# Values, queries and keys by fifteen products on thirds, in a two-layer graph kernel on one core

## The chip, the core and the metric

The kernel runs on one core of a Trainium2 chip. TensorE (PE) multiplies matrices into PSUM; VectorE (DVE) and ScalarE (ACT) read PSUM and do the element-wise work; GpSimd (POOL) does further sums in SBUF; SyncE (SP) issues most of the loads. The metric is the time of one execution on the device in microseconds (us).

## The reference, cut to what matters

The input is x of 128 graphs with 64 nodes and 768 features, and a 0/1 adjacency matrix adj of each graph. All arithmetic is in fp32. Layer 0 mixes three linear maps of the nodes by a masked attention; layer 1 is an attention with twelve heads of 64 features. Both end in a residual and a layer norm:

```python
def layer0(h, adj):
    attn = softmax(h @ h.T / sqrt(d)) * adj        # per graph; rows divided by their sums
    ctx = triu(attn, 1) @ (h @ Wl.T + bl) + diag(attn) * (h @ Ws.T + bs) + tril(attn, -1) @ (h @ Wr.T + br)
    return relu(layernorm(ctx, 1e-12) * gamma + beta)

def layer1(h, adj):
    q, k, v = (split_heads(h @ W + b) for W, b in ((Wq, bq), (Wk, bk), (Wv, bv)))
    s = q @ k.T / sqrt(64) + beta1 * adj
    s = where(adj > 0, s, -9e15)
    return merge_heads(softmax(s) @ v)

x = layernorm(x + layer0(x, adj))
x = layernorm(x + layer1(x, adj))
```

The change touches how q, k and v are computed, and how the heads are grouped in the scores and the weighted sums.

## The kernel before

**Blocks and stages.** The 8192 nodes are cut into 16 blocks of 512 tokens (8 graphs). The main loop (L1030 to L1157) runs over n. In one turn it does layer 0 of block m = n + 1, layer 1 of block n, and the end of layer 1 of block p = n - 1, which lags by one turn. TensorE's stages of a turn, in order, are: the left and right maps of block m (`both_sides`, L620, from block 3 on; "deep" below), its self map (`self_part`), then the values of block n (`values`, L774), then queries and keys of block n for three groups of four heads (`projected`, L794).

**Seven products.** A product of a 512x768 and a 768x768 matrix is done with seven products of halves in place of eight (`seven`, L370), by sums and differences of the halves of tokens and of the weights. Each of the seven is three matmuls (K is 384) for each of two halves: for the values over 128 tokens with 384 columns, for a group of queries or keys over 128 features with 256 token columns. Products accumulate in PSUM chains of the tags X and Y, two banks each; what is read halfway is kept in `u` and added at a later read. The left and right maps of deep blocks apply this twice: 49 sub-products, most of one or two matmuls of 384 columns (`nested`, L425).

**Places and queues.** Nothing is scheduled automatically: the order of every engine's instructions is the order in which the program issues them. Each product of a stage is a place; `hooks` names functions that run ahead of it. The deep stage has 28 places spread over its 49 sub-products (`left` 0 to 13, `right` 14 to 27). After each product `step` (L137) takes waiting items from three queues: `first` goes before `urgent`, that before `lazy`, and one plain item is taken per step. Items marked act or gap may come along without using that up. In the deep stage the steps behind sub-products 5, 1 and 3 of each seven are light, and take no plain item. `settle(key)` (L163) issues at once everything that is still queued up to the last item with that key; `freed` (L158) issues all that is left in `first`.

**Layer 1's attention.** `scores` (L822) issues the score matmuls of a group, multiplies by the mask on VectorE, and queues under the key ("e", n, group): adding the bias, the row maximum, lowering by it (each on 128x1024), then sixteen exponentials of 32x256 on ScalarE, and two transposes of 128x512 on VectorE. `weighted` (L876) settles that key, issues the product of the probabilities with the values, and queues four additions under ("y", n, group) in `first`. Each addition is one reciprocal and four multiply-adds of 128x64. `finish` (L907) settles ("y", n, 0) and ("y", n, 1), and queues the layer norm (L945, L946). Groups 0 and 1 have their scores within the stage of queries and keys (of group 1 and group 2); group 2 has them in the next turn's deep stage, at left 2. The weighted sums come in group 2's stage (group 0), at left 5 (group 1) and at right 1 (group 2); `finish` is at right 2.

**Loads.** Weights of the self, left, right and value stages and of queries and keys go through one ring of 19 buffers (`wst`), 192 KB each. SyncE issues a load where its product is issued in the program, so a load goes out as soon as its buffer has been read, up to 19 buffers ahead of TensorE. ScalarE issues the four loads `sq<-x1d` (L301), which bring layer 0's output back in a transposable order.

Of the kernel before, what the change touches and what calls it, by code (L numbers as in the profile page):

```python
# [17 lines left out]
P = 128  # L18
# [5 lines left out]
T = 4  # L24
# [7 lines left out]
NHG = HC  # L32
# [17 lines left out]

@with_exitstack
def gnn_two_layers(ctx: ExitStack, tc, x, adj, wl, bl, ws, bs, wr, br, gamma, beta,
# [8 lines left out]
    s_p = ctx.enter_context(tc.tile_pool(name="s_p", bufs=1))  # L61
    s2_p = ctx.enter_context(tc.tile_pool(name="s2", bufs=2))
    l0 = ctx.enter_context(tc.tile_pool(name="l0", bufs=1))
    l0t = ctx.enter_context(tc.tile_pool(name="l0t", bufs=T))
    tmp = ctx.enter_context(tc.tile_pool(name="tmp", bufs=2))
    wst = ctx.enter_context(tc.tile_pool(name="wst", bufs=19))
# [106 lines left out]
    qk_d = tc.dram_tile([NHG, 7, P, 2, HC, P], F32, name="qk_d")  # L173
# [23 lines left out]

    def prepare(nm, quarter_pool, sum_pool, waits=(0, 0, 0), queue=lazy):
# [7 lines left out]
        for q in ((0, 0), (1, 0), (0, 1), (1, 1)):  # L206
            b[q] = chunks(quarter_pool, f"b{q[0]}{q[1]}_{nm}")

            with tc.issue_after(streamed["l"][8]) if nm == "k" else ExitStack():
                move(nc.sync, b[q][1], b[q][0], source=src[q])  # L210
# [3 lines left out]
        if nm in "slrv":  # L214
            d = tc.dram_tile([4, P, HC, HALF], F32, name=f"d_{nm}")
            pieces[nm] = {1: src[0, 0], 2: src[1, 0], 3: src[1, 1], 5: d[0], 6: d[1], 7: d[2], 4: d[3]}

        def store(i):
            if nm in "slrv":
                if i in (5, 6, 7, 4):  # L220
                    move(nc.gpsimd, in_sbuf[i][1], in_sbuf[i][0], to=pieces[nm][i])
            else:


                engine, first = (nc.sync, streamed["s"][20]) if nm == "q" else (nc.gpsimd, last_sum[1].ins)
                with tc.issue_after(first):
                    for hg in range(NHG):
                        engine.dma_start(out=qk_d[hg, i - 1, :, "qk".index(nm)],
                                        in_=in_sbuf[i][1][:, :, hg * P : (hg + 1) * P])
# [25 lines left out]
        if nm in "qk":  # L255
            later(key, lambda: store(1), lambda: store(2), lambda: store(3), queue=queue)
# [60 lines left out]
    def combined(xT, n=None):  # L317

        a11, a12 = xT[:, 0:HC, 0:HTOK], xT[:, HC:KC, 0:HTOK]
        a21, a22 = xT[:, 0:HC, HTOK:NTOK], xT[:, HC:KC, HTOK:NTOK]  # L320
        s1, s2 = (s_p.tile([P, HC, HTOK], F32, tag=f"S{i}", name=f"S{i}") for i in (1, 2))
        nc.gpsimd.tensor_tensor(s1, a21, a22, ALU.add)  # L322
        nc.gpsimd.tensor_tensor(a21, a11, a21, ALU.subtract)
        S = {1: a11, 2: a12, 4: a22, 5: s1, 6: s2, 7: a21}
        if n is not None and n >= DEEP:

            S["deep"] = {i: second_level(S[i]) for i in ORDER2[:2]}
        nc.gpsimd.tensor_tensor(s2, s1, a11, ALU.subtract)
        return S

    def combined4(S, n=None):

        S[3] = s_p.tile([P, HC, HTOK], F32, tag="S4", name="S4")
        last_sum[n] = nc.gpsimd.tensor_tensor(S[3], S[2], S[6], ALU.subtract)

# [265 lines left out]

    def side_part(n, nm, in_sbuf, hooks={}):
# [3 lines left out]
        if nm == "l":  # L606
            blk["lr"] = [l0t.tile([P, 2, D], F32, tag="lr", name=f"lr_{n}_{t}") for t in range(T)]
# [12 lines left out]
    def both_sides(n, hooks):  # L620
# [4 lines left out]
        lr = blk["lr"] = [l0t.tile([P, 2, D], F32, tag="lr", name=f"lr_{n}_{t}") for t in range(T)]  # L625
# [20 lines left out]
        def view(ps):  # L646
            return ps[:, 0:HALF].rearrange("p (s c) -> p s c", s=2)

        C = {(m, n_): {(a, b): lr[2 * m + a][:, :, n_ * HALF + b * QUAD : n_ * HALF + (b + 1) * QUAD]
                       for a in range(2) for b in range(2)} for m in range(2) for n_ in range(2)}  # L650
# [4 lines left out]
        def swapped(t):  # L655
            low, high = lr[t][0:L, 1, :], lr[t][L:P, 0, :]
            swap = l1s_p.tile([P, T * 4 * L], F32, tag="s", name="swap")
# [6 lines left out]
    def context0(n):  # L664
# [8 lines left out]
        def unused():  # L673
            return l1s_p.tile([P, T * 4 * L], F32, tag="s", name="unused")[:, 0:D]
# [99 lines left out]
    def values(n, hooks={}, stay=False):  # L774

        def pairs(a):
            return a.rearrange("p (j r d) -> p r j d", r=2, d=HD)  # L780

        def last(t, h, ps, part):
            add = pairs(bias["v"][:, h * HALF : (h + 1) * HALF] if part is None else part)
            heads = slice(h * 3, (h + 1) * 3)
            nc.vector.tensor_tensor(v[:, t, :, heads, 0:HD], pairs(ps), add, ALU.add)

        by_tokens("v", blocks[n]["S"], last, None, hooks)
        if not stay:
            low, high = v[0:L, :, 1, :, 0:HD], v[L:P, :, 0, :, 0:HD]
            swap = l0t.tile([P, T, HP, HD], F32, tag="lr", name="swap")  # L790
# [3 lines left out]
    def projected(n, hg, hooks={}):  # L794

        blk = blocks[n]
        S = blk["S"]
        qk = [l1_p.tile([P, 2, NTOK], F32, tag=nm, name=nm) for nm in "qk"]
        wt = {}

        def factors(i, j):
            w = wst.tile([P, HC, P], F32, tag="w", name="wqk")
            nc.sync.dma_start(out=w, in_=qk_d[hg, i - 1, :, j])
            return [(w[:, k, :], S[i][:, k, :]) for k in range(HC)]

        def first(j, b, ps, kept):
            u = tmp.tile([P, HALF], F32, tag="u1" if kept else "u0", name="uqk")[:, 0:HTOK]
            c = b * HC + hg
            nc.scalar.activation(u, ps, AF.Identity, bias=bias["qk"[j]][:, c : c + 1])  # L809
            return u  # L810

        def last(j, m, h, ps, part):
            dst = qk[j][:, h, m * HTOK : (m + 1) * HTOK]
            if part is None:
                nc.scalar.activation(dst, ps, AF.Identity, bias=bias["qk"[j]][:, h * HC + hg : h * HC + hg + 1])  # L815
            else:
                nc.vector.tensor_tensor(dst, ps, part, ALU.add)  # L817

        seven(HTOK, factors, first, last, hooks, True)
        blk["qk"] = qk  # L820

    def scores(n, hg, at_once=1, pool=None, gaps=1):  # L822


# [3 lines left out]
        q, k = blk["qk"]  # L828
# [4 lines left out]
        s = l1s_p.tile([P, T * 4 * L], F32, tag="s", name="s").rearrange("p (t c r m) -> p t c r m", t=T, c=2, r=2)  # L833
        sc = [ps_mm.tile([P, T, 2, L], F32, tag="mm", name=f"sc{r}") for r in range(2)]
        for t in range(T):
            for c in range(2):
                for r in range(2):
                    rows = slice(r * HD, (r + 1) * HD)
                    for g in range(2):
                        tok = slice(t * P + g * L, t * P + (g + 1) * L)  # L840
                        nc.tensor.matmul(sc[r][g * L : (g + 1) * L, t, c, :], lhsT=q[rows, c, tok],  # L841
                                         rhs=k[rows, c, tok], start=True, stop=True)
        m8, add = blk["m8"], blk["add"]
        for r in range(2):
            nc.vector.tensor_tensor(s[:, :, :, r, :], sc[r], m8[:, :, None, :].to_broadcast([P, T, 2, L]), ALU.mult)
# [3 lines left out]
        mx = st.tile([P, T * 4], F32, tag="mx1", name="mx1")  # L849

        def exponentials(groups):
            if 0 in groups:
                blk["eT", hg] = (pool or l1e_p).tile([P, T, 2, P], F32, tag="lr" if pool else "eT", name="eT")
            e = blk["eT", hg].rearrange("p t c i -> p (t c) i")
# [8 lines left out]
        def turn(h):  # L863
            e = blk["eT", hg][:, h * 2 : h * 2 + 2].rearrange("p t c i -> p (t c i)")
            nc.vector.transpose(e, e)

        later(("e", n, hg),
              lambda: nc.vector.tensor_tensor(s4, s4, add[:, :, None, :].to_broadcast([P, T, 4, L]), ALU.add),
              lambda: nc.vector.tensor_reduce(mx, s8, AX.X, ALU.max),
              lambda: nc.vector.tensor_tensor(s8, s8, mx[:, :, None].to_broadcast([P, T * 4, L]), ALU.subtract),  # L870
              *(part for a in range(0, P // Q, at_once) for part in
                (act(partial(exponentials, range(a, a + at_once))), *([GAP] if hg == 1 and a == 0 else []))),
# [3 lines left out]
    def weighted(n, hg):  # L876
# [4 lines left out]
        settle(("e", n, hg))  # L881
        freed()
        xt, eT = blk["x"], blk["eT", hg]
        y = {(r, h): ps_mm.tile([P, 2, 2, HD + 1], F32, tag="mm", name=f"ps_y{r}") for h in range(2) for r in range(2)}
        for h in range(2):
            for t in range(2):
                for c in range(2):
                    for r in range(2):
                        rows = slice(r * L, (r + 1) * L)
                        for g in range(2):  # L890
                            cols = slice(g * L, (g + 1) * L)
                            nc.tensor.matmul(y[r, h][cols, t, c, :], lhsT=eT[rows, 2 * h + t, c, cols],  # L892
                                             rhs=v[rows, 2 * h + t, g, hg + c * HC, :], start=True, stop=True)

        def added(h, r):
            ps = y[r, h]
            rz = st.tile([P, 2, 2], F32, tag="rz1", name="rz1")
            nc.vector.reciprocal(rz, ps[:, :, :, HD])
            for t in range(2):
                res = xt[2 * h + t].rearrange("p (c k r d) -> p r c k d", c=2, k=HC, r=2)  # L900
                for c in range(2):
                    nc.vector.scalar_tensor_tensor(res[:, r, c, hg, :], ps[:, t, c, 0:HD], rz[:, t, c : c + 1],  # L902
                                                   res[:, r, c, hg, :], ALU.mult, ALU.add)

        later(("y", n, hg), *[partial(added, h, r) for h in range(2) for r in range(2)], queue=first)
# [386 lines left out]
```

## Time and profile before

| | us |
|---|---|
| median of three runs (2890.94 to 2893.04) | 2891.47 |
| profiled execution | 2889.82 |
| its span, first to last instruction | 2888.1 |
| VectorE's read of PSUM 128x384 (L443), mean | 0.554 |
| VectorE's multiply out of PSUM 128x512 (L845), mean | 0.684 |
| VectorE's transpose 128x512 (L865), mean | 0.701 |
| ScalarE's copy out of PSUM 128x384 (L441), mean | 0.478 |
| VectorE's reciprocal 128x4 (L898), mean | 0.172 |
| layer norm 128x768 on VectorE (L728), mean | 0.753 |

The granted TensorE clock is 0.998. The core works through a block in about 175.7 us: SyncE issues the same load of x at 1401.16 and at 1576.88. In the stretch 1360 to 1412, within a deep stage, the 16 DMA engines are busy 99% of the time, moving 282 GB/s; from 1472 to 1534, mostly queries and keys, 49% and 138 GB/s. Landing times of loads are taken from issue to landing: those of the left and right weights (L634) are 2.2, 3.8 and 10.1 us (least, median, most), those of queries and keys 2.1, 2.4 and 7.4.

A line of groups gives: line, engine, operation, output and input, shapes, count, then the busy time and the mean of one in ns, then the idle time ahead of them and what ended it. A timeline line begins with start and length in us.

### The profile page before, as it was taken

Reading aid. Unit: us, or ns where it says so; the run is one execution under the profiler, and the core shown is the slowest. Engines: PE = TensorE matmul, PEld = TensorE weight load, DVE = VectorE, ACT = ScalarE, POOL = GpSimd, SP = SyncE. Lnnn points to the kernel's source line nnn. Section 1 sums busy time; section 2 is a strip of 40 time slices with the busy share of each in tenths; the row PEclk is TensorE's granted clock in tenths of the full one; section 3 lists DMA queues with packets and bytes.
Section 4 is the critical chain, followed back from the end, with each engine's and each line's share of the span. In section 5 each row is a group of like instructions: output and inputs, shape, how many; then the busy total and the mean of one; then the engine's idle time right before and its main releaser. Section 6 shows DMA issues by size and latency. Waiting matters only on the chain.

```text
span 2888.1 us, 49913 instructions
## 1 busy us (share of the span) xinstructions
PE 2852.7 (99%) x17578; PEld 1940.3 (67%) x17578; DVE 1971.5 (68%) x3973; ACT 1121.9 (39%) x2107; POOL 717.5 (25%) x879
## 2 busy tenths in 40 slices
PE   9999999999999999999999999999999999999997
PEld 5658567585675857658576675766758667585685
DVE  6678777676676676757667576766767667676655
ACT  0004324354243443434344343443434524354254
POOL 3133123313132140412405123051230412314110
PEclk9999999999999999999999999999999999999999
DMA  9788877849578595875958669496694967849443
GB/s 342 225 269 282 251 226 199 250 141 294 155 211 242 155 283 151 235 218 167 278 143 249 198 181 273 137 281 169 191 258 140 294 159 200 250 138 295 137 127 99
DMA packets 440662, 613.18 MB, mean 212 GB/s; under 512 B 53584, under 2 KB 416720, under 8 KB 440416
## 3 DMA queue, kind: packets, MB, share of 16 engines
q1 hardware_dynamic: 362960, 495.93, 56.7%
q10 hardware_dynamic: 60848, 44.05, 8.2%
q0 software_dynamic: 16608, 70.01, 6.8%
q8 instruction: 143, 2.34, 0.3%
q14 instruction: 103, 0.84, 0.1%
HBM read 539.43 MB, written 77.27 MB: 214 GB/s over the span
## 4 chain that ended last, share of the span: by engine, by line
PE 97%; POOL 1%; issue 1%; DVE 1%; ACT 0%; DMA 0%; POOLq 0%; SPq 0%; ACTq 0%
PE ps_X L389 38%; PE ps_Y L389 28%; PE ps_Y L643 12%; PE ps_X L643 10%; PE ps_ctx L684 3%; PE sc L841 2%; PE ps_y L892 2%; PE u L532 2%; PE ps_x L291 0%; POOL q L343 0%; ACT eT L861 0%; DVE u_deep L443 0%; DMA xa<-in_x_dram 0%; POOL q L341 0%; POOL q L342 0%
## 5 line engine op out<-in xcount | busy, mean ns | idle before, releaser
L389 PE MATMUL ps_X<-xT,wqk 128*128 128x256 f32 x1728 | 391.9, 380 | 0.6 <-ACT uqk L809 0.6
L389 PEld LDWEIGHTS ps_X<-xT,wqk 128*128 128x128 f32 x1728 | 327.0, 190 | 52.9 <-ACT k L815 4.6
L861 ACT ACTIVATE eT<-s 32x256 f32<-32x256 f32 x768 | 317.8, 414 | 48.9 <-DVE s L870 38.8
L322 POOL TENSOR_TENSOR S<-hT 128x768 f32<-128x768 f32 x16 | 28.9, 1808 | 1124.1 <-PE ps_Y L389 1093.1
L389 PE MATMUL ps_Y<-S,wqk 128*128 128x256 f32 x1152 | 264.3, 379 | 0.0
L389 PEld LDWEIGHTS ps_Y<-S,wqk 128*128 128x128 f32 x1152 | 218.9, 190 | 29.8
L695 ACT ACTIVATE unused<-o 128x768 f32<-128x768 f32 x60 | 50.6, 843 | 478.7 <-DVE o L692 218.7
L643 PE MATMUL ps_Y<-wlr,q 128*128 128x384 f32 x546 | 208.6, 491 | 0.0
L443 DVE TENSOR_TENSOR lr<-ps_Y,u_deep 128x384 f32<-128x384 f32 x273 | 151.3, 554 | 70.2 <-PE ps_Y L643 41.9
L809 ACT ACTIVATE uqk<-ps_X,bq 128x256 f32<-128x256 f32 x144 | 68.1, 473 | 333.3 <-PE ps_X L389 332.5
L389 PE MATMUL ps_X<-wv,xT 128*128 128x384 f32 x576 | 195.5, 489 | 0.0
L389 PE MATMUL ps_X<-ws,hT 128*128 128x384 f32 x540 | 179.2, 486 | 0.0
L817 DVE TENSOR_TENSOR q<-ps_Y,uqk 128x256 f32<-128x256 f32 x144 | 61.0, 423 | 169.8 <-PE ps_Y L389 97.4
L420 DVE TENSOR_TENSOR u<-ps_X,bv 128x384 f32<-128x384 f32 x96 | 53.3, 555 | 165.4 <-PE ps_X L389 165.4
L389 PEld LDWEIGHTS ps_X<-wv,xT 128*128 128x128 f32 x576 | 108.0, 190 | 80.4 <-DVE o L692 8.4
L443 DVE TENSOR_TENSOR u_deep<-ps_X,lr 128x384 f32<-128x384 f32 x195 | 107.7, 552 | 77.4 <-PE ps_X L643 71.2
L902 DVE SCALAR_TENSOR_TENSOR o<-ps_y,rz,o 128x64 f32<-128x64 f32 x720 | 154.7, 277 | 6.3
L643 PE MATMUL ps_X<-wlr,q 128*128 128x384 f32 x364 | 149.1, 491 | 9.2 <-POOL q L344 6.9
L948 ACT ACTIVATE unused<-o 128x768 f32<-128x768 f32 x60 | 50.6, 843 | 266.6 <-DVE o L902 165.6
L389 PEld LDWEIGHTS ps_X<-ws,hT 128*128 128x128 f32 x540 | 102.5, 190 | 71.4
L643 PEld LDWEIGHTS ps_Y<-wlr,q 128*128 128x128 f32 x546 | 101.6, 190 | 67.2
L389 PE MATMUL ps_X<-S,wqk 128*128 128x256 f32 x576 | 138.3, 385 | 0.0
(258 smaller groups left out, 5524.4 us busy)
## 6 DMA issues: line engine op xcount, KB each, us to landing
wlr<-lr_d SPq DMA_DIRECT2D x819, 192.0 KB, 3.8
wqk<-qk_d SPq DMA_DIRECT2D x672, 192.0 KB, 2.4
wv<-d_v SPq DMA_DIRECT2D x192, 192.0 KB, 3.1
ws<-d_s SPq DMA_DIRECT2D x180, 192.0 KB, 5.8
wv<-in_L_gnn_Wv_dram SPq DMA_DIRECT2D x144, 192.0 KB, 4.1
ws<-in_L_gnn_W_self_dram SPq DMA_DIRECT2D x135, 192.0 KB, 5.6
xa<-in_x_dram SPq DMA_DIRECT2D x64, 384.0 KB, 6.1
sq<-in_x_dram ACTq DMA_DIRECT2D x56, 384.0 KB, 6.8
```

The lines of the kernel that those rows point to most:

```text
L389: nc.tensor.matmul(ps, lhsT=a, rhs=b, start=(c == 0 and i in (1, 2, 5)), stop=(c == len(fs) - 1), skip_group_check=True)
L420: recent["u"] = evicted[nm] = nc.vector.tensor_tensor(u, ps, bias[nm][:, b * HALF : (b + 1) * HALF], ALU.add)
L443: nc.vector.tensor_tensor(dst, view(ps), add, ALU.add)
L532: nc.tensor.matmul(u[g * L : (g + 1) * L, t, :], lhsT=xT[:, c, tok], rhs=xT[:, c, tok], start=(c == 0), stop=(c == KC - 1))
L643: nc.tensor.matmul(ps, lhsT=a, rhs=b, start=(k == 0 and j in (1, 2, 5)), stop=(k == len(fs) - 1), skip_group_check=True)
L684: nc.tensor.matmul(ps[g * L : (g + 1) * L, 0:HALF], lhsT=blk["aT"][:, t, g * L : (g + 1) * L], rhs=blk["lr"][t][:, g, h * HALF : (h + 1) * ...
L809: nc.scalar.activation(u, ps, AF.Identity, bias=bias["qk"[j]][:, c : c + 1])
L817: nc.vector.tensor_tensor(dst, ps, part, ALU.add)
L841: nc.tensor.matmul(sc[r][g * L : (g + 1) * L, t, c, :], lhsT=q[rows, c, tok], rhs=k[rows, c, tok], start=True, stop=True)
L861: nc.scalar.activation(e[to[0], :, to[1]], pairs[rows, :, cols], AF.Exp)
L892: nc.tensor.matmul(y[r, h][cols, t, c, :], lhsT=eT[rows, 2 * h + t, c, cols], rhs=v[rows, 2 * h + t, g, hg + c * HC, :], start=True, stop= ...
L902: nc.vector.scalar_tensor_tensor(res[:, r, c, hg, :], ps[:, t, c, 0:HD], rz[:, t, c : c + 1], res[:, r, c, hg, :], ALU.mult, ALU.add)
```

## The change

Values, queries and keys are no longer done by seven products of halves. They use fifteen products of a matrix cut into two token halves and three feature thirds with weights cut into three by three (FIFTEEN); eighteen would be the plain count. Each product is two chunks of K (256) by two halves: four matmuls of 256 columns. Ten sums of x (SUMS_X) are made by GpSimd, fifteen sums of weights (SUMS_W) once at the start, stored in DRAM and loaded from there per product.

The products accumulate in four PSUM chains of two tags. Each read takes the chain's prefix (128x512, a full bank) and adds or subtracts it in place in v or qk; the first read of a destination adds the bias. Queries and keys come in two groups of six heads: 2 x 15 products of four matmuls for three times 42. The scores of a group are handled in two halves of 128x768, the exponentials are 32x384 (still sixteen), the transposes 128x768; a weighted sum has eight additions of one reciprocal and three multiply-adds. The e chain of a group now has six VectorE items for three.

The hooks move: scores(p, 1) at left 1, weighted(p, 0) at left 4, weighted(p, 1) at right 1, and `finish` stays at right 2 (deep blocks). No weighted sum is left in the stage of queries and keys. The ring `wst` has 12 buffers of 192 KB for 19, and a ring `wh` of 4 buffers of 256 KB serves values, queries and keys; `eT` has one buffer for two. The last block's sums are by sixths (`sixth`) for quarters.

```diff
+FIFTEEN = ((3, 16, 3, ((1, 2, -1),)), (4, 3, 2, ((1, 0, 1), (1, 1, -1))), (7, 15, 1, ((1, 1, 1),)),
...
+CHAIN_TAG = ("Y", "X", "Y", "X")
...
-    wst = ctx.enter_context(tc.tile_pool(name="wst", bufs=19))
...
+    def products(width, factors, taken, hooks, stage):
+        bank, seen = {}, set()
+        for place, (x, w, chain, reads) in enumerate(FIFTEEN):
+            for f in hooks.get(place, ()):
+                f()
+            start = chain not in bank
+            if start:
+                tag = CHAIN_TAG[chain]
+                bank[chain] = ps_st.tile([P, 2, width], F32, tag=tag, name=f"ps_{tag}")
+            ps = bank[chain]
+            fs = factors(place, x)
+            for h in range(2):
+                for k, (a, b) in enumerate(fs[h]):
+                    nc.tensor.matmul(ps[:, h, :], lhsT=a, rhs=b, start=start and h == 0 and k == 0,
+                                     stop=k == len(fs[h]) - 1, skip_group_check=True)
+            for i, j, sign in reads:
+                taken(i, j, sign, ps, (i, j) not in seen)
+                seen.add((i, j))
+            step()
...
+        def taken(i, j, sign, ps, first):
+            dst = qk[:, :, j, i * HTOK : (i + 1) * HTOK]
+            if first:
+                for h in range(2):
+                    c = 2 * j + m
+                    nc.scalar.activation(dst[:, h], ps[:, h, :], AF.Identity, bias=bias["qk"[h]][:, c : c + 1],
+                                         scale=float(sign))
+            else:
+                nc.vector.tensor_tensor(dst, dst, ps, ALU.add if sign > 0 else ALU.subtract)
...
+        def added(h):
+            ts = slice(2 * h, 2 * h + 2)
+            nc.vector.tensor_tensor(s4[:, ts], s4[:, ts], add[:, ts, None, :].to_broadcast([P, 2, 6, L]), ALU.add)
+        def largest(h):
+            nc.vector.tensor_reduce(mx[:, h * 12 : (h + 1) * 12], s8[:, h * 12 : (h + 1) * 12], AX.X, ALU.max)
+        def lowered(h):
+            part = slice(h * 12, (h + 1) * 12)
+            nc.vector.tensor_tensor(s8[:, part], s8[:, part], mx[:, part, None].to_broadcast([P, 12, L]), ALU.subtract)
...
-        later(("y", n, hg), *[partial(added, h, r) for h in range(2) for r in range(2)], queue=first)
+        def added(h, r, t):
+            ps = y[h, r]
+            rz = st.tile([P, THIRDS], F32, tag="rz1", name="rz1")
+            nc.vector.reciprocal(rz, ps[:, t, :, HD])
+            res = xt[2 * h + t].rearrange("p (j r d) -> p r j d", j=KC, r=2)
+            for c in range(THIRDS):
+                nc.vector.scalar_tensor_tensor(res[:, r, 2 * c + m, :], ps[:, t, c, 0:HD], rz[:, c : c + 1],
+                                               res[:, r, 2 * c + m, :], ALU.mult, ALU.add)
+        later(("y", n, m), *[partial(added, h, r, t) for h in range(2) for r in range(2) for t in range(2)], queue=first)
...
+    wst = ctx.enter_context(tc.tile_pool(name="wst1", bufs=12))
+    wh_p = ctx.enter_context(tc.tile_pool(name="wh", bufs=4))
...
-            at(one, 2, scores, p, 2, *((1,) if last else (2, None, 4)))
-            at(one, 5, weighted, p, 1)
+            at(one, 1, scores, p, 1, *((1,) if last else (2, None, 4)))
+            at(one, 4, weighted, p, 0)
             if not last and m < DEEP:
-                at(left, 13, weighted, p, 2)
+                at(left, 13, weighted, p, 1)
                 at(right, 0, finish, p)
             elif not last:
-                at(right, 1, weighted, p, 2)
+                at(right, 1, weighted, p, 1)
                 at(right, 2, finish, p)
```

## The prediction

> **What bounds the kernel now.** I read the busy shares first, then the chain that ended last, then the pace of single matmuls in TensorE's timeline, and last one score group followed through three engines.
>
> ```profile
> PE 2852.7 (99%) x17578; PEld 1940.3 (67%) x17578; DVE 1971.5 (68%) x3973; ACT 1121.9 (39%) x2107; POOL 717.5 (25%) x879
> PE 97%; POOL 1%; issue 1%; DVE 1%; ACT 0%; DMA 0%; POOLq 0%; SPq 0%; ACTq 0%
> ```
>
> TensorE works 99% of the span, and 97% of the final chain is its own. Two things follow: each microsecond of matmul taken away is a microsecond of time, and each new wait of TensorE is added in full, since there are no gaps that it could share.
>
> ```profile
> 1412.58 4.03 PE L389 MATMUL ps_X<-ws,hT 128*128 128x384 f32 x12
> 1416.45 4.03 PE L389 MATMUL ps_Y<-ws,hT 128*128 128x384 f32 x12
> ...
> 1500.36 2.75 PE L389 MATMUL ps_X<-S,wqk 128*128 128x256 f32 x12
> 1502.95 2.75 PE L389 MATMUL ps_Y<-S,wqk 128*128 128x256 f32 x12
> ```
>
> The columns are start, length, then the group. An fp32 matmul leaves two records, so twelve are six matmuls. From start to start six of 384 columns take 1416.45 - 1412.58 = 3.87 us, 0.645 us each; six of 256 columns take 1502.95 - 1500.36 = 2.59 us, 0.432 us each. These two prices carry the gain.
>
> The third score group of a graph block, where the kernel now has time to spare:
>
> ```profile
> 1545.15 1.22 DVE L870 TENSOR_TENSOR s<-s,mx 128x1024 f32<-128x1024 f32 x1
> ...
> 1555.78 0.70 DVE L865 STREAM_TRANSPOSE eT<-eT 128x512 f32<-128x512 f32 x1
> ...
> 1557.95 0.70 DVE L865 STREAM_TRANSPOSE eT<-eT 128x512 f32<-128x512 f32 x1
> ```
> ```profile
> 1546.41 5.11 ACT L861 ACTIVATE eT<-s 32x256 f32<-32x256 f32 x12 [2.04 <-DVE s L870]
> 1551.43 0.32 ACTq L301 DMA_DIRECT2D sq<-x1d  x1
> 1551.53 1.70 ACT L861 ACTIVATE eT<-s 32x256 f32<-32x256 f32 x4
> 1558.83 4.54 ACTq L301 DMA_DIRECT2D sq<-x1d  x3
> ```
> ```profile
> 1563.87 1.16 PE L892 MATMUL ps_y<-v,eT 64*64 64x65 f32 x64
> ```
>
> The scores are lowered by their maximum until 1546.37, sixteen exponentials follow on ScalarE until 1553.23, two transposes on VectorE until 1558.65, and TensorE takes up the product with the values at 1563.87: 5.2 us of reserve, and no wait.
>
> ```profile
> L861 ACT ACTIVATE eT<-s 32x256 f32<-32x256 f32 x768 | 317.8, 414 | 48.9 <-DVE s L870 38.8
> L902 DVE SCALAR_TENSOR_TENSOR o<-ps_y,rz,o 128x64 f32<-128x64 f32 x720 | 154.7, 277 | 6.3
> wlr<-lr_d SPq DMA_DIRECT2D x819, 192.0 KB, 3.8
> ```
>
> These rows give an exponential's price, that of a weighted sum's addition, and the landing time of the left and right weights (median 3.8 us).
>
> **What the Trainium skill says.** "PSUM — Partial Sum Buffer", section "Engine vs sequencer instructions": the queues of ScalarE and VectorE are strict FIFO, and matmuls start and complete in program order. The case rests on this: an instruction emitted late can't be overtaken on its way. The trace agrees; the third exponential run stood behind a load that ScalarE issued at 1551.43. "ScalarE: Activation LUTs", section "What ACT_TABLE_LOAD costs": about 0.833 ns per further element of an ACTIVATE. No run before has exponentials of 384 elements, so I estimate 414 + 128 x 0.833 = 521 ns. The trace agrees nearly: 0.48 us for a copy of 384 and 0.84 us for an ACTIVATE of 768 give 0.94 ns per element. "TensorE: Matmul & The Clock Gate", section "Wait — 56ns, not 53.3ns?": N / 2.4 GHz plus 2.5 ns per matmul pass; four passes of 256 are an estimated 437 ns, against 432 measured.
>
> **The products.** Values: 7 x 2 x 3 = 42 matmuls of 384 columns become 15 x 4 = 60 of 256: 42 x 0.645 = 27.09 us become 60 x 0.432 = 25.90, so -1.19. Queries and keys: 126 x 0.432 = 54.39 become 2 x 60 x 0.432 = 51.80, so -2.59. Scores and weighted sums keep 96 small matmuls each. Gain 3.78 us per block, 60.5 us in sixteen.
>
> **Reads of the chains.** A prefix is read in full banks of 128x512. VectorE has none for this shape and place before, but its multiply out of PSUM of the same size takes 0.684 us (L845). Values: 14 x 0.555 = 7.8 us become 16 x 0.684 = 10.9; queries and keys: 18 x 0.42 (L817) = 7.6 become 20 x 0.684 = 13.7, beside 24 reads on ScalarE before and after. A product is 4 x 0.432 = 1.73 us long, and a chain mostly comes up again two products, 3.45 us, later. One read and one queued item of at most 1.1 us fit into 1.78 us, near balance; I take 0, between 0 and 0.05 x 45 = 2.2 us per block. POOL's ten-odd sums of 128x512 (some 1.3 us each, between 128x384 at 1.0 and 128x768 at 1.83) lie ahead in the self stage: 0.
>
> **The deep ring.** Left and right weights have 12 buffers for 19. A load then starts about 5.2 to 7.7 us before its first use (counted in products between a buffer's last reader and its next) instead of 11 to 15. The median landing is 3.8 us, the slowest quarter 5.4 and more, and the DMA queues are 99% busy in such a stage. Alone I would price it at 1 to 4 us per block; behind the wait that follows, in which loads catch up, I take 0.5 (0 to 2).
>
> **The second score group.** This decides. In the order of the changed program's instructions, scores(p,1) are multiplied just after left place 1. Each heavy step then takes one plain item, and the queue of the weighted sums goes first: two e items, then eight additions of weighted(p,0) (before: four per group), then the rest of the group. The second half of "lowered" comes out behind the reads of deep sub-product 24, three 384-column matmuls (1.9 us) ahead of weighted(p,1); there the settle call empties the chain at once. So on every engine directly before the weighted product stand: lowered, 16 exponentials, 2 transposes.
> VectorE gets, from the first score multiply to the end of lowered: 20 reads x 0.555 = 11.1, 4 multiplies x 0.555 = 2.2, 6 e items of 768 elements x about 0.95 = 5.7, 4 norms x 0.75 = 3.0, 8 additions x (0.17 + 3 x 0.215) = 6.6; 28.6 us, in a stretch of TensorE's work of 24.9 us, ending 1.9 us before the weighted product. So lowered ends 28.6 - 24.9 - 1.9 = 1.8 us past the moment when TensorE could start. Then 16 x 0.52 = 8.3 us of exponentials and 2 transposes of 128x768, each about 1.0 us (0.70 for 512): TensorE waits 1.8 + 8.3 + 2.0 = about 12 us, in part before the stage's last products. Low end: no lag of VectorE, exponentials at the old 0.414: 0.95 - 1.9 + 6.6 + 1.4 = 7. High end: 15, if the loads issued by ScalarE ahead of the exponentials (the three of the fence lasted to 1563.37) hold them up 3 us more.
>
> **The burst behind it.** finish(p) one place later settles the additions of groups 0 and 1. Before, the last group was number 2 and trickled out between reads; now it is number 1 and all eight additions, 6.6 us, are put on VectorE in one piece ahead of the next reads. PSUM holds two banks per tag, two sub-products of up to 1.3 us each per chain: TensorE waits about 6.6 - 2.6 = 4 us (2 to 6).
>
> **Sum.** Per deep block (n = 2 to 14, thirteen): 12 + 4 + 0.5 - 3.8 = +12.7, so +165 us. Block 1: its chain also ends at the weighted product, +12 - 3.8 = +8. Block 0: -3.8. Last block: exponentials of both last groups stand 3.6 to 5 us ahead, some +5 each, less 3.8: +6. Together +175. The profiled execution took 2889.82 us, 1.7 us below the median; so 2891.5 + 175 = 3066 us.
>
> **Rivals.**
> The products win: the decision point is a wait plus burst under 3.8 us per deep block. It needs VectorE and ScalarE to reach the second group's exponentials 12 us sooner than I count, because queued items leave faster than one per heavy step. For it: 99% busy TensorE makes 60.5 us of matmul certain. Against it: the order of instructions. With 2 us left of the waits: 2891 - 60 + 13 x 2 = 2857 us.
> The weights starve: the score chain hides, but the ring of 12 costs 1 to 4 us per block, the stage being at 99% DMA: 2891 - 60 + 13 x 2.5 = 2863; at 5 us it would be 2896, no gain. Against it: median landing 3.8 us is below the lead of 5.2.
> All add up: the ScalarE loads hold the exponentials 3 us, the ring costs 2, VectorE's balance 1 more: 3066 + 13 x 6 = 3144 us.
> Only the exponentials: the burst hides in two banks and the wait is 7 to 8: 2891 + 13 x (7.5 - 3.8) + 10 = 2950.
>
> **How the numbers follow.** Forecast case 0.62; all add up 0.17; exponentials only 0.12; products win or starve 0.09. A change under 0.2% (5.8 us) is what a measurement of this kernel can't tell from none. Slower 0.91, same 0.01, faster 0.08. The range takes the forecast's bounds (13 x -5 to 13 x +6) and most of the two slower cases: 2955 to 3145.
>
> **What would show it.** Right: TensorE idle of about 12 us per block before the weighted product of the second group, released by the transpose or an exponential; a second gap of about 4 us right behind, released by VectorE reads, with a run of additions in VectorE's timeline; 256-column products at 0.432 us; PE busy near 2790 us. Wrong: those products with gaps between them, or TensorE's idle time put down to the weights' loads, or no gap at the weighted product.

## The result, and the profile after

The changed kernel takes 3282.41 us (median of four runs, 3280.43 to 3287.26) against 2891.2 us before: a ratio of 1.1356, interval 1.1336 to 1.1375. The direction was forecast, the size was not: 3066 us, with 3145 as the upper end. The profiled execution has a span of 3285.4 us, 397 us more than before.

The page of the changed kernel, busy shares and then the chain that ended last:

```profile
PE 2888.7 (88%) x17962; PEld 2057.0 (63%) x17962; DVE 2122.4 (65%) x4190; ACT 1049.4 (32%) x1849; POOL 835.1 (25%) x999
PE 67%; DMA 12%; issue 5%; ACT 5%; POOL 3%; DVE 2%; SPq 0%; ACTq 0%; POOLq 0%
```

TensorE is idle for 12% of the span, where it had 1%. It is also busy 36 us longer than before, although it has some 60 us less to multiply. That can't come from the work; the granted clock, 0.943 for 0.998, says where to look.

TensorE's waits from 794.3 to 3012.8, which are eleven periods of the deep blocks (line; what it waited for; us in all, how often, the longest; `issue` stands where the profile names nothing that was waited for):

```profile
PE ps_y L1025 <- DVE eT L999: 124.4, 11, 11.8
PE ps_X L752 <- issue: 46.8, 22, 4.1
PE ps_X L752 <- DMA wlr<-lr_d: 43.3, 13, 5.2
PE ps_X L488 <- DMA ws<-in_L_gnn_W_self_dram: 31.0, 25, 3.1
PE ps_Y L752 <- DMA wlr<-lr_d: 5.5, 10, 1.5
```

One such block, TensorE (start, length, group, in brackets the idle time ahead and what ended it), then ScalarE and VectorE:

```profile
1565.04 1.32 PE L752 MATMUL ps_X<-wlr,q 128*128 128x384 f32 x2 [3.68 <-DMA wlr<-lr_d]
1577.77 2.88 PE L1025 MATMUL ps_y<-v,eT 64*64 64x65 f32 x96 [11.41 <-DVE eT L999]
...
1592.28 1.25 PE L752 MATMUL ps_X<-wlr,q 128*128 128x384 f32 x2 [4.09 <-issue]
```
```profile
1551.32 15.49 ACTq L357 DMA_DIRECT2D sq<-x1d  x4
1566.90 1.28 ACT L995 ACT_TABLE_LOAD   x1 [23.70 <-DMA wlr<-lr_d]
1568.19 8.51 ACT L995 ACTIVATE eT<-s 32x384 f32<-32x384 f32 x16
```
```profile
1560.22 1.49 DVE L978 TENSOR_TENSOR s<-s,mx 128x768 f32<-128x768 f32 x1
...
1576.73 1.84 DVE L999 STREAM_TRANSPOSE eT<-eT 128x768 f32<-128x768 f32 x2 [9.19 <-ACT eT L995]
...
1589.92 0.67 DVE L1034 SCALAR_TENSOR_TENSOR o<-ps_y,rz,o 128x64 f32<-128x64 f32 x3
1590.51 0.55 DVE L542 TENSOR_TENSOR lr<-ps_X,lr 128x384 f32<-128x384 f32 x1
```

The reader sees the forecast chain: lowering ends at 1561.71, the exponentials run from 1568.19 to 1576.70, the transposes to 1578.57, and TensorE stands still for 11.41 us, since its first weighted matmul needs only the first transpose. Before, the transposes were done 5.2 us ahead. Then the eight additions, which end at 1590.59, keep the reads of PSUM waiting and TensorE with them for 4.09 us. Two things are not as forecast. Between lowering and exponentials ScalarE waited 5.2 us in issuing the `sq<-x1d` loads and loaded a table for 1.28. And the weights came 3.68 us late. The two are tied: the last of the four issues goes out at 1566.50, just after a weight load has landed at 1566.48.

The clock in the same block (columns: window, its length, busy time of PE, PEld, DVE, ACT and POOL, the granted clock, DMA share, GB/s):

```profile
1560.00:1565.00 5.00, 0.91 (x2) 0.30 (x2) 1.72 (x2) 0.00 (x0) 2.03 (x3) 1.00 1.08 230
1565.00:1566.00 1.00, 0.96 (x2) 0.30 (x2) 0.00 (x0) 0.00 (x0) 0.00 (x0) 0.68 1.06 373
1566.00:1577.00 11.00, 0.35 (x1) 0.00 (x0) 1.38 (x3) 9.61 (x17) 0.00 (x0) 0.50 0.48 131
1577.00:1582.00 5.00, 4.23 (x98) 3.52 (x99) 1.57 (x2) 0.00 (x0) 0.00 (x0) 0.50 0.00 0
1582.00:1583.00 1.00, 1.00 (x4) 0.66 (x3) 0.56 (x1) 0.00 (x0) 0.04 (x1) 0.79 0.00 0
...
1593.00:1596.00 3.00, 3.00 (x6) 1.49 (x6) 1.67 (x3) 2.90 (x7) 2.05 (x3) 0.50 0.32 81
```

Some 4 us after TensorE fell idle (at 1561.36) its clock halves, and in this block it stays halved for almost 5 us after work has come back. So a part of the wait is paid a second time: the weighted product takes 2.88 us where the same 96 records of the first group took 1.63, and the sub-products behind it run at half speed too. After the 4.09 us gap the same happens again, for some 3.5 us.

The sum for one deep period. It lasts (3012.8 - 794.3) / 11 = 201.7 us for (2641.1 - 691.2) / 11 = 177.3 before, +24.4:

| term | measured, us per block | forecast |
|---|---|---|
| wait at the weighted product, 124.4 / 11 | 11.3 | 12 |
| gap behind VectorE's additions (`issue`), 46.8 / 11 | 4.25 | 4 |
| left and right weights, (43.3 + 5.5) / 11 | 4.4 | 0.5 |
| self weights, 31.0 / 11 | 2.8 | none |
| matmuls at the lowered clock | 6.1 | none |
| the products | -3.8 | -3.8 |
| sum, less 0.7 for small gaps (0.9 before, 0.2 after) | 24.3 | 12.7 |

The clock's term is worked out from TensorE's busy time: 1964.85 us in these eleven periods, against 1939.72 - 11 x 3.78 = 1898.1 that it should have been; 66.7 / 11 = 6.1. The -3.8 in it is taken from the forecast, so that the table's sum closes by its making. Run e12 below tests both terms: it does the same products at full clock and is busy for 1899.5 us in eleven periods, which makes 5.9 us for the clock and -3.7 for the products. By the starts of layer 0's score matmuls, the fourth block's come 52.8 us later than before (467.1 for 414.3), and from the last block's to the end it takes 396.6 us for 346.2. The end alone has three waits behind the score chain: 9.1, 10.1 and 4.9 us.

### The profile page after: what moved, and what is told of

Same layout as the page of the kernel before. It is cut to its first block, busy times and chain, and to the rows that moved or that the text cites. A ratio compares the mean times of both kernels' runs of the same rounds, so it can differ in the third digit from the quotient of the medians.

```text
span 3285.4 us, 49861 instructions
## 1 busy us (share of the span) xinstructions
PE 2888.7 (88%) x17962; PEld 2057.0 (63%) x17962; DVE 2122.4 (65%) x4190; ACT 1049.4 (32%) x1849; POOL 835.1 (25%) x999
## 4 chain that ended last, share of the span: by engine, by line
PE 67%; DMA 12%; issue 5%; ACT 5%; POOL 3%; DVE 2%; SPq 0%; ACTq 0%; POOLq 0%
PE ps_X L428 21%; PE ps_Y L428 14%; PE ps_X L488 7%; PE ps_Y L752 7%; PE ps_X L752 6%; DMA wlr<-lr_d 5%; PE ps_Y L488 5%; DMA ws<-in_L_gnn_W_self_dram 4%; ACT eT L995 4%; PE ps_ctx L800 2%; PE ps_y L1025 2%; PE sc L957 1%; DMA sq<-x1d 1%; PE u L631 1%; ACT L995 1%
## 5 line engine op out<-in xcount | busy, mean ns | idle before, releaser
L995 ACT ACTIVATE eT<-s 32x384 f32<-32x384 f32 x512 | 266.5, 520 | 97.6 <-DVE s L978 91.4
L488 PE MATMUL ps_X<-ws,hT 128*128 128x384 f32 x540 | 202.7, 527 | 38.5 <-DMA ws<-in_L_gnn_W_self_dram 36.9
L428 PE MATMUL ps_X<-xT,wqk 128*128 128x256 f32 x1024 | 234.5, 379 | 1.9 <-DVE w_deep L332 1.9
L1025 PE MATMUL ps_y<-v,eT 64*64 64x65 f32 x2880 | 68.0, 267 | 171.5 <-DVE eT L999 162.4
L428 PEld LDWEIGHTS ps_X<-xT,wqk 128*128 128x128 f32 x1024 | 194.5, 190 | 29.0 <-DVE w_deep L332 2.2
L936 DVE TENSOR_TENSOR qk<-qk,ps_X 128x512 f32<-128x512 f32 x160 | 109.8, 686 | 123.9 <-PE ps_X L428 63.2
L428 PE MATMUL ps_Y<-more,wqk 128*128 128x256 f32 x768 | 181.5, 379 | 0.2 <-DMA wqk<-qk_d 0.2
L428 PE MATMUL ps_X<-sums,wqk 128*128 128x256 f32 x768 | 181.5, 383 | 0.0
L936 DVE TENSOR_TENSOR qk<-qk,ps_Y 128x512 f32<-128x512 f32 x160 | 109.1, 682 | 105.7 <-PE ps_Y L428 104.3
L752 PEld LDWEIGHTS ps_X<-wlr,q 128*128 128x128 f32 x364 | 67.8, 199 | 167.0 <-issue 115.7
L428 PEld LDWEIGHTS ps_Y<-more,wqk 128*128 128x128 f32 x768 | 145.8, 190 | 20.3 <-DVE w_deep L332 0.5
```

Of the source, the lines that this page charges most:

```text
L428: nc.tensor.matmul(ps[:, h, :], lhsT=a, rhs=b, start=start and h == 0 and k == 0, stop=k == len(fs[h]) - 1, skip_group_check=True)
L488: nc.tensor.matmul(ps, lhsT=a, rhs=b, start=(c == 0 and i in (1, 2, 5)), stop=(c == len(fs) - 1), skip_group_check=True)
L752: nc.tensor.matmul(ps, lhsT=a, rhs=b, start=(k == 0 and j in (1, 2, 5)), stop=(k == len(fs) - 1), skip_group_check=True)
L936: nc.vector.tensor_tensor(dst, dst, ps, ALU.add if sign > 0 else ALU.subtract)
L995: nc.scalar.activation(e[to[0], :, to[1]], pairs[rows, :, cols], AF.Exp)
L1025: nc.tensor.matmul(y[h, r][cols, t, c, :], lhsT=eT[rows, 2 * h + t, c, cols], rhs=by_parity[rows, 2 * h + t, 2 * c + m, g, :], start=True, ...
```

## The experiments

Two theories stood. The chain theory: score items leave the queue too late, the rest follows. The ring theory: with 12 buffers for 19 the weights starve TensorE. A third came up on the way, that the loads `sq<-x1d` collide with the ring.

**e1, e2, e3: the score chain.** e1 lets the last group's additions trickle out; e2 gives the queue as many items as before the change; e3 does both.

```diff
# e1, in finish
         settle(("y", n, 0))
-        settle(("y", n, 1))
# e2, in scores and weighted
-              *[partial(f, h) for f in (added, largest, lowered) for h in range(2)],
+              *[lambda f=f: (f(0), f(1)) for f in (added, largest, lowered)],
...
-        later(("y", n, m), *[partial(added, h, r, t) for h in range(2) for r in range(2) for t in range(2)], queue=first)
+        later(("y", n, m), *[lambda h=h, r=r: (added(h, r, 0), added(h, r, 1)) for h in range(2) for r in range(2)], queue=first)
```

> The changed kernel (3282 us), but finish settles group 0's additions only; the last group's eight additions leave the queue one per step. Chain theory: the 4.25 us gap behind the weighted product and the low clock after it (about 1.5 us) go in each of 13 deep blocks: about 3282 - 75 = 3207 us, the 11 us wait at the weighted product stays. Ring theory (12 buffers are the main cost): what TensorE gains here it waits for weights instead: 3250 or more.

> The changed kernel, but the six VectorE items of a score group leave the queue as three pairs, and the eight additions as four pairs, as many steps as before the change; no instruction added or removed. Chain theory: the exponentials end some 14 us of TensorE's work ahead of the weighted product, its wait of 11.3 us goes and with it about 3.5 us of low clock: 13 x 14.8 = -190, about 3090 us; the burst behind it stays. Ring theory: the waits for weights (4.4 left and right, 2.8 self, per block) grow by about what is saved: 3180 or more.

> Both edits at once, the pairs and the shorter settle. Chain theory: the wait at the weighted product (11.3 us per deep block), the burst (4.25) and the low clock behind them (about 5) all go: 13 x 20.5 = -267, about 3015 us, with the 7 us of waits for weights left. Ring theory: the waits for weights take the place of the others, 3150 us or more.

Measured: e1 3148.77 us (1.0889 of before, 1.0873 to 1.0905), e2 3069.40 (1.0634, 1.0592 to 1.0676), e3 2972.43 (1.0284, 1.025 to 1.0318). TensorE's waits in e1:

```profile
PE ps_y L1025 <- DVE eT L999: 176.3, 14, 15.1
PE ps_X L752 <- DMA wlr<-lr_d: 35.3, 17, 3.8
```

In e1 the gap behind the additions is gone and the wait at the product stands, as the chain theory says. The gain was larger, 134 us for 75. The self weights' wait is gone with it: in the changed kernel finish's output stores are issued 2.8 to 4.4 us after the loads of x, among the first self weights, which then land after 7 to 10 us; in e1 the stores come 11.7 us after the first of these, and the same weights land after 5 to 7. TensorE's busy time fell by 51 us (2888.7 to 2837.9): the clock. So the burst cost 134 / 13 = 10.3 us per block: 4.25 of its own, 2.8 of self weights, and the rest mostly clock. That the stores make the self weights late is read from these times; no run moves the stores alone. In e2 the wait at the product does not occur in the deep blocks; one of 1.1 us, at 344.79 in the start, is all that is left of it:

```profile
PE ps_y L1025 <- DVE eT L999: 1.1, 1, 1.1
```

With it 213 us go, again more than the forecast 190. Both together take 310 us: the placing of two queues' items is most of the 391 us. e3 is still 82 us slower than before, and the ring theory's value of 3150 is far off as the main cause.

**e4: the ring by itself.** The kernel before, with 12 buffers (`bufs=19` to `bufs=12`).

> The kernel before (2891 us), with a ring of 12 weight buffers for 19 and nothing else. Chain theory: 1 to 2 us per deep block, 2905 to 2917 us. Ring theory: the 7.2 us per block that the changed kernel waits for left, right and self weights, and more from a lowered clock: 2985 us or more.

Measured 2965.78 us (1.0258, 1.0239 to 1.0278): +75 us, between the two values and nearer to the ring theory's. Its waits:

```profile
PE ps_Y L643 <- DMA wlr<-lr_d: 19.5, 20, 2.4
PE ps_X L389 <- DMA ws<-in_L_gnn_W_self_dram: 10.7, 12, 1.3
```

All of TensorE's waits come to 63 us for 21 before; the rest is TensorE busy for 25 us more (2877.8 for 2852.7), of which the granted clock, 0.996 for 0.998, explains only a part. The ring is a cost of its own on an otherwise unstalled kernel: by layer 0's score matmuls a deep block takes (2607.3 - 604.1) / 11 = 182.1 us for 177.3, 4.8 more.

**e6: one more buffer** (13 for 12, and 3 for 4 in the other ring).

> Pairs and shorter settle (2972 us) with 13 buffers in the weight ring and 3 for 4 in the ring of values, queries and keys. Theory of the size: the lead grows by 1/12, about 0.6 us, which takes at most that off each of two gaps and their low clock: about 2972 - 13 x 1.5 = 2952 us. Theory of the collision: a landing of 9 us is still far beyond the lead: 2965 us or more. Should the ring of 3 starve (lead 3.45 us against a median landing of 2.6), it is slower than 2972.

Measured 2973.2 us, the same as e3. The waits for left and right weights did not shrink (15.6 us for 14.7), and what the self weights gained (3.5 for 10.3) the weights of values, queries and keys lost in their smaller ring (15.4 for 3.2). Moving one buffer brings nothing; a thirteenth without taking one away was not run.

**e5, e7, e8: the loads of layer 0's output moved.** In e3 a weight load that took 3 us takes 5 to 9 while these four loads are under way.

```diff
-                when, place = (left, 10) if n > 1 else (right, 2)
+                when, place = (right, 7) if n > 1 else (right, 2)
```

> Pairs and shorter settle (2972 us) with the four loads of layer 0's output that ScalarE issues (sq<-x1d, 8 to 10 us each) moved from left 10 to 13 to right 7 to 10, behind most of the deep stage's weights. Theory of the collision: these loads slow the weights' loads from about 3 to 9 us and a ring of 12 can't cover that; away from them the two gaps of about 2 us per block, and the low clock behind them, go: 13 x 6 = -78, about 2894 us. Theory of the size: 12 buffers are too few at 99% DMA share in any case: 2955 us or more.

> The changed kernel (3282 us) with only those four loads moved to right 7 to 10. In its trace the exponentials stand behind the four issues on ScalarE, from the end of lowering at 1561.7 until 1566.8. If the queue on ScalarE is a part of the wait, the wait at the weighted product falls from 11.3 to about 8 and the wait for weights ahead of it (4.4) goes: 13 x 8 = -100, about 3180 us. If the late items alone make the wait, it stays: 3260 us or more.

> The kernel before with a ring of 12 (2966 us) and those four loads moved in the same way. Theory of the collision: about 2900 us, most of the 75 us comes back. Theory of the size: 2950 us or more.

Measured: e5 3078.67 us (+106 on e3), e8 3058.04 (+92 on e4), e7 3255.66 (27 less than the changed kernel, for the expected 100). The waits for left and right weights nearly vanish (in e8 from 24.8 us to 2.4, in e7 from 57.5 to 2.6): with these loads out of the way, 12 buffers almost suffice in the deep stage. But the move made a new wait. TensorE, VectorE and ScalarE in e8:

```profile
1677.72 1.62 PE L643 MATMUL ps_X<-wlr,q 128*128 128x384 f32 x2 [10.11 <-issue]
```
```profile
1676.31 0.18 DVE L931 RECIPROCAL f<-f 128x4 f32<-128x4 f32 x1 [11.26 <-ACT f L928]
```
```profile
1664.28 10.47 ACTq L301 DMA_DIRECT2D sq<-x1d  x2
1674.78 1.28 ACT L928 ACT_TABLE_LOAD   x1 [12.48 <-DMA sq<-x1d]
```

The cause is ScalarE's queue. At right 7 to 10 the issues fall among the steps of the layer norm at the end of layer 1. The third load goes out only at 1674.44, when the second has landed at 1674.42. Behind it stands the norm's square root with its table load; VectorE's reciprocal waits 11.26 us for that root, and the reads of PSUM stand behind the reciprocal. In e5 the same reciprocal waits 9.74 us. The transposes of the loaded rows, named in the expectations of e9 and e10, are not what TensorE waits for: it is back at work at 1677.72, and the fourth load lands at 1681.08. So e5 and e8 do not price the collision: what the weights gained is hidden behind a new wait of another kind. e7 tells what the loads do on ScalarE's queue at their old place:

```profile
1550.36 1.50 DVE L978 TENSOR_TENSOR s<-s,mx 128x768 f32<-128x768 f32 x1
...
1561.78 1.84 DVE L999 STREAM_TRANSPOSE eT<-eT 128x768 f32<-128x768 f32 x2 [8.86 <-ACT eT L995]
```
```profile
1551.94 1.28 ACT L995 ACT_TABLE_LOAD   x1 [18.61 <-DVE s L978]
1553.23 8.51 ACT L995 ACTIVATE eT<-s 32x384 f32<-32x384 f32 x16
```

The exponentials now follow lowering at once, and yet the wait is still 161.2 us in 14. Late weights had covered that part of the chain: TensorE now arrives earlier by what the chain is shorter. The loads on ScalarE and the late weights cost the same 4 to 5 us, not both; and of the 55 us that the left and right weights no longer cost, 27 come back as waits for self weights (63.8 us for 36.9), beside which the loads now stand. The rest, 28, is close to the 27 measured. So neither theory's value was met.

**e9, e10, e11: where else the loads can stand.** e9 and e11 spread them over left 10, left 13, right 2 and right 5 (on e3 and on e4); e10 puts them at right 3 to 6 (on e3).

> Pairs and shorter settle (2972 us) with the four loads of layer 0's output spread over left 10, left 13, right 2 and right 5, so that mostly one is under way at a time. Theory of the collision: the weights' landings rise to 5 to 6 us in place of 9, the two gaps of 2 us and their low clock shrink: about 13 x 4 = 52 us less, 2920 us. Theory of the size: 2960 us or more. If VectorE's transposes come to wait for the last load, as when all four went to right 7, a gap opens at the start of the self stage.

> Pairs and shorter settle (2972 us) with the four loads at right 3 to 6. In the run with right 7 the weights' waits were gone, and VectorE's transposes waited 10 us for the fourth load; four places (about 7 us) earlier most of that wait goes: 3079 - 13 x 8 = about 2975 us, or less if the weights' waits stay away (2930). Theory of the size: the gaps only move, 2970 us or more.

> The kernel before with a ring of 12 (2966 us) and those four loads spread in the same way. Theory of the collision: more than half of the 75 us comes back, 2925 us or less. Theory of the size: 2955 us or more.

Measured: e9 2949.6 us, 23 less than e3; e11 2941.56, 24 less than e4; e10 2999.02. Spreading gives back a third of the ring's 75 us, less than the collision theory's half. In e11 it takes the waits for self weights (1.9 us for 12.5), while those for left and right weights stay (27.1 for 24.8). With e8, where these vanished, both are causes: 12 buffers are short when these loads stand among the weights', whether together or spread. e10 met ScalarE's queue once more: VectorE waits 5.27 us for a step of the same norm, and TensorE has gaps of about 3 us. In e9 one gap of 2 us per block stays, at the same place. VectorE and TensorE there:

```profile
1602.50 0.97 DVE L999 STREAM_TRANSPOSE eT<-eT 128x768 f32<-128x768 f32 x1
1603.39 0.52 DVE L542 TENSOR_TENSOR lr<-ps_Y,u_deep 128x384 f32<-128x384 f32 x1
1604.01 0.56 DVE L542 TENSOR_TENSOR u_deep<-ps_X,lr 128x384 f32<-128x384 f32 x1
```
```profile
1604.67 0.89 PE L752 MATMUL ps_X<-wlr,q 128*128 128x384 f32 x2 [2.04 <-issue]
```

TensorE goes on 0.1 us after VectorE has read the bank; VectorE has had no gap since 1584.17. So at this place `issue` hid a bound on VectorE, not a load.

**e12: the repairs joined.** e9, with the loads of x moved from right 8 to 11 to own 4 to 7 (places of the self stage), the second group's transposes three queue steps later, and half of the first block's ten sums on VectorE.

> The spread version (2950 us) with three more moves: the loads of x for the residual go out at own 4 to 7 in place of right 8 to 11, away from the first self weights; the second group's transposes come three queue steps later, out of the stretch in which VectorE works without a gap from 1583 to 1605; half of GpSimd's ten sums of x at the start of layer 1 are made by VectorE, once. If the waits that its trace shows at these places are their own (2.1 us per block for self weights, 2.0 behind VectorE, 7.5 and low clock at the start): 2950 - 13 x 4 - 12 = about 2886 us, level with the kernel before. If the gaps only move on, 2930 us or more.

Measured 2915.16 us (1.0083, 1.0067 to 1.01), 29 above the hoped 2886. From 626.2 to 2567.2, eleven periods by layer 0's score matmuls, against the kernel before from 591.6 to 2541.9:

```profile
626.20:2567.20 1941.00, 1899.51 (x12257) 1362.89 (x12256) 1441.92 (x2816) 753.86 (x1310) 562.63 (x682) 1.00 0.71 207
```
```profile
591.60:2541.90 1950.30, 1940.13 (x11993) 1315.31 (x11992) 1335.19 (x2696) 802.75 (x1486) 498.11 (x616) 1.00 0.73 209
```

At full clock TensorE is busy 40.6 us less in eleven blocks, 3.7 each for the forecast 3.8: the gain of the products is real. A deep block is 0.85 us shorter than before; small waits, 3.7 us per block for 0.9, eat the rest, and 2.4 of them are for GpSimd's sums `q` in the deep stage (0.5 before). The kernel is slower all the same, since its start is 35.9 us longer (450.2 for 414.3).

**e13, e14: the start.** Fifteen of the thirty stores of key weights that GpSimd issues at the start went to ScalarE, in the changed kernel and in e12.

> The changed kernel (3282 us) with the 15 stores of the second group's key weights issued by ScalarE in place of GpSimd. If GpSimd's issues hold up the first block's sums, the wait for them (6 us and low clock after it) goes: about 3272 us, and the third attention of layer 0 starts about 10 us earlier. If VectorE's sums of weights or the loads are the cause, 3280 us or more.

> The joined version (2915 us) with the same change of stores: 2905 us if GpSimd's issues hold up the start, 2913 us or more if not. Below the kernel before (2890) only if the start's other gaps (weights of queries and keys just stored, 4.8 us) went with it.

Measured: e13 3282.3 us and e14 2913.93 us (1.0084, 1.007 to 1.0097): no change. The first sums of x began 1.2 us earlier in e14 than in e12, no more (215.23 for 216.43). GpSimd's issues are not the cause. VectorE's first sum in e12, which has no stores to issue, begins at 216.46 as well, after 7.95 us of waiting for a store of key weights to land. What makes these late, and the start longer, stays open. No version ran faster than the kernel before.

## Why the prediction was right in kind and wrong in size

The wait of the second score group, the burst and the products came in about the sizes forecast, the first in part by luck. What failed are terms of the sum: the clock behind each wait (taken at nothing, about 6 us per block), the deep ring (0.5, measured 4.4), the self weights (no term, 2.8), and the start and the end.

- **The products.** Forecast -3.78 us per block. Right: a product takes 1.73 us in the trace, and e12 has 3.7 us less busy time per block.
- **The second score group.** Forecast 12 us, from 7 to 15; measured 11.3, and e2 shows that the items' order is its cause. The sum was right by luck in part. TensorE waited for one of the two transposes, about 1.0 us of the 2.0 counted. VectorE was not the 1.8 us behind that were counted: in e7, where TensorE is not late, lowering ended 0.4 us after it could have started (1551.86 against 1562.81 - 11.38). In its place stood a table load of 1.28 us, which no step had, and in the changed kernel what the high end had named, ScalarE's loads; of these the late weights covered nearly all. That such a load holds exponentials up does not follow from the line at 1551.43 that the prediction names, since they went on at 1551.53 without a pause; the changed kernel shows it. The exponentials, estimated at 0.521 us from "ScalarE: Activation LUTs", section "What ACT_TABLE_LOAD costs", have a mean of 520 ns.
- **The burst behind it.** Forecast 4 us, measured 4.25; e1 shows the cause. The step missed what `finish` brings forward, its output stores, and with them (by their times) 2.8 us per block of late self weights, which e1 removed. That "each new wait of TensorE is added in full" also stopped at the wait itself.
- **The clock.** No step had it: about 6 us per deep block (5.9 against e12), some 80 us in thirteen. Its own sign, TensorE busy near 2790 us, was missed by 99. The profile before could not show it, since TensorE never stood for more than a microsecond in its deep blocks; that the price of a wait was taken as its length is the largest single error.
- **The deep ring.** The term "I take 0.5 (0 to 2)" was mis-sized: 4.4 us. It rested on the median landing of 3.8 us against a lead of 5.2. The profile before also had 10.1 us as the longest landing, and in e3 the late ones come together, beside the `sq<-x1d` loads; e4 prices the ring at 75 us on the kernel before. That loads "catch up" in the wait was no help, since the starving comes ahead of it.
- **Reads of the chains** were taken at 0 and cost little in e12: one wait of 0.3 us behind VectorE and one of 0.4 behind ScalarE per block.
- **Start and end.** Forecast +8 - 3.8 and +6; measured +52.8 to the fourth block's scores and +50.4 from the last one's to the end, of which some 24 are one deep block's. In the start 15.1 us are the same score wait in the first turn; some 36 us remain in e12. There TensorE is idle for 37.0 us where it was 7.7, in many waits of up to 6.6 us, and busy for 6.6 us more; why was not found.
- **Together**: thirteen blocks with 11.7 us more than forecast make 152 us; start and end are about the rest of the 216. The rival in which all adds up (3144 us) had the ring and ScalarE's loads, and was still short, for want of the clock and the start. The faster rivals needed waits under 3.8 us per block; the trace has six times that (22.8).

## What to carry to other kernels

When work is regrouped so that fewer, larger groups each queue more items, count the queue's steps up to the first reader: a drain call turns every missing step into a wait. Price a wait of TensorE of several microseconds at its length and the half-speed matmuls behind it, here about a quarter more (6 us on 22.8). Size a load ring against the slowest landings that come in a row, not against the median. Look at what stands behind a load on the queue of a computing engine: where its issue has to wait, as for 10 us in e8, all that follows waits too.

## What the runs showed of the hardware

In the block shown the clock fell some 4 us after TensorE went idle, and came back almost 5 us after it had work; with the 4.09 us gap it fell just as work resumed. Neither time is fixed: in a block of e1 the clock was full again within 3.5 us of work (work from 1513.54, half clock until 1516, full from 1517). A gap of 2.02 us in e3 was followed by half clock for about 3 us, one of 2.04 us in e9 by none, so a gap's length alone does not tell. The table load ahead of the exponentials was not done in ScalarE's idle time: in e7 ScalarE had been idle for 18.61 us, and the load began only when lowering had ended, so its 1.28 us lie on the chain.
